# Key and query weights of a second attention, loaded and centred among the experts of the layer before it

## The chip, the cores and the metric

The kernel runs on one core of one Trainium2 chip. The metric is the device time of one execution in microseconds (us); of several runs the median is taken. A profile of one execution, taken by the hardware profiler, goes with the times.

## The reference

A two-layer perceiver block on float32 data: 8 samples of 64 latent rows of 512, and a context of 1601 rows of 512 for each sample. Six steps are added to x one after the other.

```python
x = x + L0_xattn(layernorm(x), ctx)     # 16 heads of 64 over 1601 context rows
x = x + L0_attn(layernorm(x))           # Fourier chunks, attention, convolutions
x = x + L0_ffn(layernorm(x))            # 8 experts, each token goes to one
x = x + L1_xattn(layernorm(x), ctx)     # 16 heads of 32 over 1601 context rows
x = x + L1_attn(layernorm(x))           # relative positions
x = x + L1_ffn(layernorm(x))            # ternary weights, 8 bit levels
```

The change lies in the third and the fourth step, with a trace in the fifth:

```python
# L0_ffn: the expert of the largest router logit, at most 128 tokens an expert
h   = gelu(layernorm(tok @ W1[e] + b1[e]) * g + b)      # 512 -> 2048
out = h @ W2[e] + b2[e]                                  # 2048 -> 512
# L1_xattn: queries and keys are normalised in each head of 32
qh = layernorm32(q @ Wq.T + bq) * q_gamma + q_beta
kh = layernorm32(ctx @ Wk.T + bk) * k_gamma + k_beta
x  = softmax(qh @ kh.T / sqrt(32)) @ (ctx @ Wv.T + bv) @ Wp.T + bp
```

## The kernel before

The kernel is written with a framework that allocates memory in pools and draws all semaphores itself. A pool is a stack-like stretch of the on-chip memory; a tile of a pool is written when the earlier users of its place are done. Pools opened later in the program take over the places of pools closed before. The framework also lays out the order of the instructions on each engine, so that the order in the source gives precedence and not the place. All stages run one after the other on the core, each in its own function.

`l0_ffn` is the layer of experts. Tokens are normalised, projected (`xf`, L1051) and routed. Each token's slot number is `key` (L1087); an indirect DMA from GpSimd writes the tokens to their slots in memory (`slots`, L1092). `gather(e)` (L1101) fetches the tokens of expert e, turned into columns (`tok`): for expert 0 by a matmul of `xf` with a comparison of slot numbers (L1116, L1119), for all others by reading `slots` and transposing (L1111, L1113). `Hidden` holds one expert's work: `block` (h_ps, L1139) makes 512 of the 2048 hidden columns, `norm` and `turn` normalise and transpose them, `out` (oe_ps, L1166) is the second matmul, whose result goes to `done` (L1171). The loop over `E_` = 8 experts runs the blocks of expert e + 1 beside the transposes and the output of expert e. `Experts.load(e)` issues the weights of an expert on SP, eight DMAs of 1 MB, into six places for w1 (four in pool `experts`, two in `c_m`) and four for w2; it is called two experts ahead. After the loop `done` is gathered back into `o` by four indirect DMAs (L1198), normalised and added to x (L1206).

`l1_xattn` is the second attention. Its pools are, from the bottom: `d_e` (`ep`: the key weight wk, its bias bk, the centring matrix c_center, and kT0), `d_c` (`cp`: five places for chunks of the transposed context), `d_sq` (`qp`: four squares), `d_v` (`vp`: the value weight wv), `d_w` (`wp`: small constants, among them c_heads, the output weight wo, the queries qb, kT1 to kT3, the values v), and more. The context of a sample comes in four chunks `CK` of 384, 384, 384 and 449 columns. Because every head's keys are normalised, the mean of each head's 32 output columns is taken out of the weights beforehand: `center_weights` (L1212) does it with three VectorE instructions for each quarter of a weight (sum L1218, scale L1219, subtract L1220). `project_keys` (k_ps, L1312) makes the keys of 128 columns, one pass for each of four column blocks c: ScalarE writes them to kT and their squares to a place of `d_sq`, and `deviations` sums the squares by head with c_heads (sum_ps, L1334) and takes the power -1/2 on GpSimd. Keys go through two PSUM banks (`d_ps_m`). After the keys of sample 0 the bias of the output is completed (bo_ps, L1365), then the queries are made (q_ps, L1385) from wq and bq, which are loaded and centred in pool `d_q`. Then come eight rounds, one for each sample: scores, softmax, values of this sample (v_ps, L1413), keys of the next, the weighted sum (acc) and, every second round, the output (out_ps, L1492).

`l1_tail` does the fifth and sixth step. Its pools `e_e` and `e_w` lie where the pools of the second attention were; its first weights are L1a_Wq, L1a_Wk and L1a_Wv (in `e_e`) and L1a_Wo (in `e_w`), all issued at L1688.

Of the kernel before, what the change touches and what calls it, by code (L numbers as in the profile page):

```python
# [21 lines left out]
P = 128  # L22
# [980 lines left out]
        self.held[e] = w1, w2  # L1003


def l0_ffn(K, x, d, experts, slots, done):

# [5 lines left out]
    with ExitStack() as es:  # L1013
# [87 lines left out]
        def gather(e):  # L1101

            b1 = rp.tile([P, HID], F32, tag="b1", name="b1")
            b2 = rp.tile([P, D], F32, tag="b2", name="b2")
            nc.scalar.dma_start(b1, bcast_rows(d["L0f_b1"][e]))
            nc.scalar.dma_start(b2, bcast_rows(d["L0f_b2"][e]))
            tok = rp.tile([P, DC, CAP], F32, tag="tok", name="tok")
            ps = pm.tile([P, DC, CAP], F32, tag="mm", name="tok_ps")
            rows = rp.tile([P, NT, P], F32, tag="rows", name="rows")
            if e:  # L1110
                nc.scalar.dma_start(rows, slots[ts(e, CAP), :].rearrange("p (c n) -> p c n", n=P))  # L1111
                for c in range(DC):
                    nc.tensor.transpose(ps[:, c, :], rows[:, c, :], K.ident)  # L1113
            else:
                for t in range(NT):
                    nc.vector.tensor_scalar(rows[:, t, :], slot, key[:, t : t + 1], None, ALU.is_equal)  # L1116
                for c in range(DC):
                    for t in range(NT):
                        nc.tensor.matmul(  # L1119
                            ps[:, c, :], lhsT=xf[:, t, ts(c, P)], rhs=rows[:, t, :], start=t == 0, stop=t == NT - 1  # L1120
                        )
            nc.vector.tensor_copy(tok, ps)
            return tok, b1, b2
# [54 lines left out]
        now.norm()  # L1178
        for e in range(E_):
            experts.load(e + 2)  # L1180
            then = Hidden(e + 1, after) if e + 1 < E_ else None
            for n in range(4):
                if then:
                    then.block(n)
                if n:
                    now.turn(n - 1)
            now.turn(3)
            if e + 2 < E_:
                after = gather(e + 2)
            if then:  # L1190
                then.norm()
            now.out()
            now = then
# [26 lines left out]
        nc.vector.tensor_sub(w3, w3, m.unsqueeze(2).to_broadcast([P, 16, DH]))  # L1220


def scale_heads(K, pool, y):

    nc = K.nc
    y3 = y.rearrange("p (h e) -> p h e", e=DH)
    sq = pool.tile([P, D], F32, tag="hl_sq", name="hl_sq")
    v = pool.tile([P, 16], F32, tag="hl_v", name="hl_v")
    r = pool.tile([P, 16], F32, tag="hl_r", name="hl_r")
    nc.scalar.activation(sq, y, AF.Square)  # L1230
    nc.vector.tensor_reduce(v, sq.rearrange("p (h e) -> p h e", e=DH), AX.X, ALU.add)
    K.root(pool, r, v, 1.0 / DH, EPS, v)
    nc.vector.tensor_mul(y3, y3, r.unsqueeze(2).to_broadcast([P, 16, DH]))
# [2 lines left out]
CK = [(0, 384), (384, 384), (768, 384), (1152, NKV - 1152)]  # L1236


def l1_xattn(K, x, d, in_last):

# [6 lines left out]
    with ExitStack() as es:  # L1247
# [11 lines left out]
        def weight(pool, name, shape, src):  # L1259
            t = pool.tile(shape, F32, tag=name, name=name)  # L1260
            nc.sync.dma_start(t, src)
# [5 lines left out]
        def load(b, i):  # L1267
            k0, n = CK[i]
            t = cp.tile([P, DC, CK[-1][1]], F32, tag="ctxT", name="ctxT")
# [33 lines left out]
        nc.tensor.matmul(ps, lhsT=center, rhs=bk, start=True, stop=True)  # L1303
        nc.vector.tensor_copy(bk, ps)

        def project_keys(ctxT, c, r):
# [61 lines left out]
        nc.vector.tensor_add(bo, bo, ps)  # L1368

        with tc.tile_pool(name="d_q", bufs=1) as tq, tc.tile_pool(name="d_l", bufs=2) as lp:  # L1370
            wq = chunked(tq, "L1x_WqT")
            bq = weight(tq, "L1x_bq", [P, D], bcast_rows(d["L1x_bq"]))
            xn = tq.tile([P, NT, D], F32, tag="xn", name="xn")
            xT = tq.tile([P, DC, B * S], F32, tag="xT", name="xT")

            nc.vector.tensor_scalar(ln[:, 0:2], ln[:, 0:2], ln[:, 2:3], DH**-0.5, ALU.mult, ALU.mult)
            center_weights(K, lp, wq, "hl_m")
            center_weights(K, lp, bq.unsqueeze(1), "hl_m")
            K.layernorm(lp, x, xn, functools.partial(K.root, lp))
            K.tokens_to_columns(ps_t, "t", xn, xT)  # L1380
            q = tq.tile([P, NT, D], F32, tag="q", name="q")
            for t in range(NT):
                ps = ps_m.tile([P, D], F32, tag="mm", name="q_ps")
                for c in range(DC):
                    nc.tensor.matmul(ps, lhsT=xT[:, c, ts(t, P)], rhs=wq[:, c, :], start=c == 0, stop=c == DC - 1)  # L1385
                nc.vector.tensor_add(q[:, t, :], ps, bq)
                scale_heads(K, lp, q[:, t, :])
                nc.vector.tensor_add(x[:, t, :], x[:, t, :], bo)
            for c in range(DC):
                ps = ps_t.tile([P, B * S], F32, tag="t", name="qT_ps")  # L1390
                for t in range(NT):
# [258 lines left out]
def l1_tail(K, x, d, w, known):  # L1650
# [324 lines left out]
def program(tc, d):  # L1975
    nc = tc.nc
    with tc.tile_pool(name="const", bufs=1) as cp, tc.tile_pool(name="memory", bufs=1, space=DRAM) as memory:
        K = Ctx(tc, cp)
        x = cp.tile([P, NT, D], F32, tag="x", name="x")
        nc.sync.dma_start(x[:, 0, :], d["x"][:P])  # L1980
        w = TernaryWeights(K, cp, memory, d)
        slots, done = (memory.tile([CAP * E_, D], F32, tag=n, name=n) for n in ("slots", "done"))
        l0_xattn(K, x, d, w)
        with tc.tile_pool(name="experts", bufs=4) as ep:
            experts = Experts(K, ep, d)
            wg = cp.tile([P, DC, E_], F32, tag="L0f_Wg", name="L0f_Wg")

            def loads():
                for e in range(1, E_):
                    nc.sync.dma_start(slots[ts(e, CAP), :], d["c_zero"])  # L1990
                experts.load_projection(wg)
                experts.load(0)

            l0_attn(K, x, d, loads)
            l0_ffn(K, x, d, experts, slots, done)
        known = []
        with tc.tile_pool(name="early", bufs=NT - 1) as sp:
            l1_xattn(K, x, d, lambda: known.extend(K.statistics(sp, x[:, t : t + 1, :]) for t in range(NT - 1)))
            l1_tail(K, x, d, w, known)


# [91 lines left out]
```

## Time and profile before

| What | Value |
|---|---|
| Time, median of 3 runs | 3249.63 us (3246.26 to 3250.2) |
| Profiled execution, own time | 3247.4 us |
| Its span | 3245.6 us |
| TensorE (PE) busy | 3118.5 us, 96% |
| VectorE (DVE) busy | 1751.6 us, 54% |
| GpSimd (POOL) busy | 995.1 us, 31% |
| ScalarE (ACT) busy | 848.7 us, 26% |
| DMA over the span | 336.87 MB, 104 GB/s |

The span holds, in order: the first attention to about 1500 us, the Fourier step to 1600, the experts to 1891, the second attention to about 3085, and the last two steps. In the lists of the profile PE is TensorE's matmul, PEld its loading of weights, SP the engine that issues most DMAs; SPq and ACTq are the queues of issuing instructions. "a <- b" in a list of waits reads: a waited for b. A float32 matmul shows as two records. L1312 is line 1312 of the kernel before. The granted clock (PEclk) is the share of full speed that TensorE was allowed.

### The profile page before, as it was taken

What the parts mean: (1) busy time and instruction counts of PE and PEld (TensorE: products, weight loads), DVE (VectorE), ACT (ScalarE), POOL (GpSimd) and SP (SyncE); (2) the same over time, 40 slices, a digit from 0 to 9 for tenths busy, and PEclk for the clock granted to TensorE, in tenths of its full rate; (3) what the DMA queues carried; (4) which work ended last, traced back from release to release, by engine and by line L of the source; (5) the groups of instructions that cost most, each with busy time, mean ns of one, the idle gap of its engine ahead of it and who ended that gap; (6) DMA issues with size and microseconds to landing.
All of it is one profiled execution on the core that took longest, in us unless ns stands there. A gap on an engine that the chain in (4) does not pass through costs nothing.

```text
span 3245.6 us, 39977 instructions
## 1 busy us (share of the span) xinstructions
PE 3118.5 (96%) x15601; PEld 2116.0 (65%) x15601; DVE 1751.6 (54%) x2918; ACT 848.7 (26%) x1583; POOL 995.1 (31%) x973
## 2 busy tenths in 40 slices
PE   8999999999999999999989979999999999999986
PEld 7777788888877888887344434556565555655553
DVE  5745565656566656653432345644546454454746
ACT  3232232222223222221112222323232232323323
POOL 5433325445444445440000023123141322403011
PEclk9999999999999999999989989999999999999998
DMA  8254553333455333326279650010101001000160
GB/s 261 77 170 140 157 166 113 102 93 101 137 169 160 102 126 98 106 85 215 75 268 343 236 179 20 22 31 11 41 1 41 20 22 41 1 31 1 40 137 14
DMA packets 316881, 336.87 MB, mean 104 GB/s; under 512 B 35541, under 2 KB 235733, under 8 KB 315429
## 3 DMA queue, kind: packets, MB, share of 16 engines
q1 hardware_dynamic: 310320, 316.72, 31.1%
q10 hardware_dynamic: 5733, 15.50, 1.4%
q8 instruction: 124, 2.03, 0.3%
q0 software_dynamic: 640, 2.10, 0.2%
q14 instruction: 64, 0.52, 0.0%
HBM read 308.02 MB, written 28.08 MB: 104 GB/s over the span
## 4 chain that ended last, share of the span: by engine, by line
PE 88%; DVE 5%; DMA 4%; ACT 2%; issue 1%; POOL 0%; SPq 0%; ACTq 0%; POOLq 0%; DVEq 0%
PE k_ps L1312 11%; PE v_ps L1413 11%; PE x_ps L581 10%; PE x_ps L466 9%; PE z_ps L581 4%; PE s_ps L1427 4%; PE z_ps L466 4%; PE oe_ps L1166 3%; PE h_ps L1139 3%; PE acc L1477 3%; PE y_ps L581 2%; PE y_ps L466 2%; PE sum_ps L1334 2%; PE s_ps L459 2%; DMA w_out<-wq 1%
## 5 line engine op out<-in xcount | busy, mean ns | idle before, releaser
L1349 POOL TENSOR_TENSOR r<-r,minus_half 128x24 f32<-128x24 f32 x64 | 288.7, 4515 | 712.9 <-DVE r L1345 699.9
L1312 PE MATMUL k_ps<-ctxT,L1x_WkT 128*128 128x384 f32 (+1 forms) x1024 | 381.5, 515 | 16.5 <-DVE L1x_WkT L1220 14.7
L1413 PE MATMUL v_ps<-L1x_WvT,ctxT 128*128 128x512 f32 (+1 forms) x832 | 375.0, 598 | 0.0
L466 PE MATMUL x_ps<-qt,ctxT 128*128 128x256 f32 x1152 | 286.3, 382 | 6.4 <-DVE s L431 5.1
L1312 PEld LDWEIGHTS k_ps<-ctxT,L1x_WkT 128*128 128x128 f32 x1024 | 186.0, 192 | 160.8 <-issue 46.9
L581 PE MATMUL x_ps<-pt,ctx 128*128 128x256 f32 x1152 | 280.3, 381 | 2.4 <-DVE a L559 1.3
L1413 PEld LDWEIGHTS v_ps<-L1x_WvT,ctxT 128*128 128x128 f32 (+1 forms) x832 | 148.3, 186 | 169.2 <-issue 163.4
L466 PEld LDWEIGHTS x_ps<-qt,ctxT 128*128 128x128 f32 x1152 | 216.9, 190 | 47.6 <-DVE s L431 9.2
L581 PEld LDWEIGHTS x_ps<-pt,ctx 128*128 128x128 f32 x1152 | 216.5, 189 | 36.0 <-DVE a L556 1.6
L137 POOL TENSOR_TENSOR ctxT<-ctxT 128x256 f32<-128x256 f32 x96 | 76.6, 798 | 405.8 <-DMA ctxT<-in_ctxT 367.7
L1427 PEld LDWEIGHTS s_ps<-qb,kT 64*128 64x128 f32 x1664 | 143.4, 187 | 74.4 <-DVE s L1439 44.4
L447 DVE TENSOR_TENSOR m<-m,s 128x512 f32<-128x512 f32 x176 | 134.6, 765 | 94.7 <-ACT s L445 92.1
L137 POOL TENSOR_TENSOR ctx<-ctx 128x256 f32<-128x256 f32 x96 | 72.5, 755 | 346.4 <-DMA ctx<-in_ctx 290.7
L1427 PE MATMUL s_ps<-qb,kT 64*128 64x128 f32 x1664 | 170.5, 287 | 7.0 <-DVE s L1439 6.8
L1316 ACT ACTIVATE kT<-k_ps,L1x_bk 128x384 f32<-128x384 f32 (+1 forms) x128 | 75.9, 593 | 356.8 <-PE k_ps L1312 343.5
L1345 DVE TENSOR_SCALAR r<-sumT_ps 128x12 f32<-128x12 f32 (+1 forms) x128 | 16.5, 166 | 252.0 <-PE sumT_ps L1342 251.7
L1416 ACT COPY v<-v_ps 128x512 f32<-128x512 f32 (+1 forms) x104 | 60.5, 582 | 330.5 <-PE v_ps L1413 330.5
L1439 DVE TENSOR_TENSOR s<-s_ps,r 128x512 f32<-128x512 f32 x192 | 124.7, 683 | 32.1 <-PE s_ps L1427 31.7
L499 DVE TENSOR_TENSOR s<-s,top_ps 128x1024 f32<-128x1024 f32 (+1 forms) x112 | 123.3, 1137 | 20.5 <-PE top_ps L489 20.5
L1468 DVE TENSOR_TENSOR s<-s,top_ps 128x1664 f32<-128x1664 f32 x64 | 117.9, 1884 | 27.6 <-PE top_ps L1464 27.6
L1447 DVE TENSOR_TENSOR fold<-s 128x1536 f32<-128x1536 f32 x64 | 112.1, 1751 | 37.5 <-ACT s L1469 37.4
L431 DVE SCALAR_TENSOR_TENSOR s<-y_ps,bias,p 128x256 f32<-128x256 f32 x96 | 46.3, 482 | 140.6 <-PE y_ps L466 140.4
(416 smaller groups left out, 5664.4 us busy)
## 6 DMA issues: line engine op xcount, KB each, us to landing
w<-in_L0f_W SPq DMA_DIRECT2D x64, 1024.0 KB, 7.5
ctxT<-in_ctxT SPq DMA_DIRECT2D x192, 256.0 KB, 4.6
ctx<-in_ctx SPq DMA_DIRECT2D x192, 256.0 KB, 3.2
ctxT<-in_ctxT SPq DMA_DIRECT2D x24, 768.0 KB, 4.4
wvT<-in_L0x_WvT SPq DMA_DIRECT2D x16, 1024.0 KB, 8.0
qk<-qk_all SPq DMA_DIRECT2D x15, 1024.0 KB, 7.1
qk_all<-stage SPq DMA_DIRECT2D x32, 384.0 KB, 3.4
wraw<-in_L1f_w1T SPq DMA_DIRECT2D x16, 512.0 KB, 4.3
```

Of the source, the lines that this page charges most:

```text
L137: nc.gpsimd.tensor_add(q[:, 4, :], q[:, 2, :], q[:, 3, :])
L447: nc.vector.tensor_max(self.m, self.m if k else self.s[:, LAST, :], self.s[:, k, :])
L466: nc.tensor.matmul(ps, lhsT=ctxT[i][:, Quarters.LEFT[n], ts(e, P)], rhs=right[n][:, e, :], start=start and e == 0, stop=e == 1, skip_group ...
L499: nc.vector.tensor_sub(s[:, k : k + n], s[:, k : k + n], top.unsqueeze(1).to_broadcast([P, n, HALF]))
L581: nc.tensor.matmul(ps, lhsT=ctx[pair][:, Quarters.LEFT[n], ts(m, P)], rhs=right[n][:, i, :], start=start and i == 0, stop=i == 2, skip_gro ...
L1312: nc.tensor.matmul(ps[:, :n], lhsT=wk[:, e, ts(c, P)], rhs=ctxT[i][:, e, :n], start=e == 0, stop=e == DC - 1)
L1349: nc.gpsimd.tensor_tensor(r[:, at : at + n, :], r[:, at : at + n, :], minus_half[:, :n, :], ALU.pow)
L1413: nc.tensor.matmul(ps[:kn], lhsT=ctxT[i][:, c, ds(at, kn)], rhs=wv[:, c, :], start=c == 0, stop=c == DC - 1)
L1427: nc.tensor.matmul(pair[j][:, i, :], lhsT=kT[c][rows, ts(k0 + i, P)], rhs=qb[rows, c, b].rearrange("p h q -> p (h q)"), start=True, stop=True,
L1439: nc.vector.tensor_mul(out, in_, by)
L1447: nc.vector.tensor_tensor(t, s[:, :, 0:6, :], s[:, :, 6:12, :], op)
L1468: nc.vector.tensor_sub(s[:, j], s[:, j], ps[:, j, :].unsqueeze(1).to_broadcast([P, NK, P]))
```

## The change

A new class `Ahead` holds the key weight, its bias, the centring matrix, the query weight, its bias and the first two chunks of sample 0's context, in two pools that lie at the other end of the on-chip memory (`side="right"`): `keys` and `queries`. They are opened before the layer of experts. At expert 1 its `load` issues seven DMAs on SP, and at expert 3 its `center` centres wk, wq and bq. In the second attention nothing of this is loaded or centred; the first two chunks are read by the first keys from `queries`, and loaded a second time into `d_c`, after chunks 2 and 3, because the values need them later. The pool `queries` is closed after the queries are made, `keys` before the last steps.

With that go three smaller edits. `gather` makes the tokens of expert 1 by matmul as those of expert 0, so that slots of experts 0 and 1 are not zeroed. In `d_w`, kT1 to kT3 are placed first and qb before wo. The pools `e_e` and `e_w` of the last steps are opened with `reuse_waits="tile"`, which lets a tile wait for the tiles whose places it takes; the default is the pool, which waits for all pools whose memory it reaches.

```diff
-            if e:
+            if e > 1:
                 nc.scalar.dma_start(rows, slots[ts(e, CAP), :].rearrange("p (c n) -> p c n", n=P))
...
                 for t in range(NT):
-                    nc.vector.tensor_scalar(rows[:, t, :], slot, key[:, t : t + 1], None, ALU.is_equal)
+                    nc.vector.tensor_scalar(
+                        rows[:, t, :], slot, float(CAP * e), key[:, t : t + 1], ALU.add, ALU.is_equal
+                    )
...
             experts.load(e + 2)
+            if e == 1:
+                ahead.load()
+            if e == 3:
+                ahead.center()
...
+class Ahead:
+    def __init__(self, K, d, keys, queries):
+        self.K, self.d, self.pool, self.queries = K, d, keys, queries
+
+    def load(self):
+        nc, d = self.K.nc, self.d
+
+        def weight(pool, name, shape, src):
+            t = pool.tile(shape, F32, tag=name, name=name)
+            nc.sync.dma_start(t, src)
+            return t
+
+        def chunks(src):
+            return src.rearrange("(c p) n -> p c n", p=P)
+
+        self.wk = weight(self.pool, "L1x_WkT", [P, DC, D], chunks(d["L1x_WkT"]))
+        self.bk = weight(self.pool, "L1x_bk", [P, DC], d["L1x_bk"])
+        self.across = weight(self.pool, "c_center", [P, P], d["c_center"])
+        self.wq = weight(self.queries, "L1x_WqT", [P, DC, D], chunks(d["L1x_WqT"]))
+        self.bq = weight(self.queries, "L1x_bq", [P, D], bcast_rows(d["L1x_bq"]))
+        self.ctxT = [
+            weight(self.queries, f"ctxT{i}", [P, DC, n], chunks(d["ctxT"][0, :, k0 : k0 + n])) for i, (k0, n) in enumerate(CK[:2])
+        ]
+
+    def center(self):
+        for w in self.wk, self.wq, self.bq.unsqueeze(1):
+            center_weights(self.K, self.pool, w, "mean")
...
-def l1_xattn(K, x, d, in_last):
+def l1_xattn(K, x, d, ahead, queries_done, in_last):
...
-        wk = chunked(ep, "L1x_WkT")
-        bk = weight(ep, "L1x_bk", [P, DC], d["L1x_bk"])
-        center = weight(ep, "c_center", [P, P], d["c_center"])
-        ctxT = [load(0, i) for i in range(4)]
+        wk, bk = ahead.wk, ahead.bk
+        ctxT = [place() for _ in range(4)]
+        for i in (2, 3, 0, 1):
+            load(0, i, ctxT[i])
+        kT = [(wp if c else ep).tile([P, NK * P], F32, tag=f"kT{c}", name="kT") for c in range(DC)]
         sel = weight(wp, "c_heads", [P, 64], d["c_heads"])
...
+        qb = wp.tile([P, DC, B, 2, S], F32, tag="qb", name="qb")
         wo = chunked(wp, "L1x_Wp")
         bo = weight(wp, "L1x_bp", [P, D], bcast_rows(d["L1x_bp"]))
-
-
-        qb = wp.tile([P, DC, B, 2, S], F32, tag="qb", name="qb")
-        kT = [(wp if c else ep).tile([P, NK * P], F32, tag=f"kT{c}", name="kT") for c in range(DC)]
...
-        center_weights(K, ep, wk, "mean")
         ps = ps_t.tile([P, DC], F32, tag="t", name="bk_ps")
-        nc.tensor.matmul(ps, lhsT=center, rhs=bk, start=True, stop=True)
+        nc.tensor.matmul(ps, lhsT=ahead.across, rhs=bk, start=True, stop=True)
...
-            project_keys(ctxT, c, r_of[c])
+            project_keys(ahead.ctxT + ctxT[2:], c, r_of[c])
...
-            wq = chunked(tq, "L1x_WqT")
-            bq = weight(tq, "L1x_bq", [P, D], bcast_rows(d["L1x_bq"]))
+            wq, bq = ahead.wq, ahead.bq
...
-            center_weights(K, lp, wq, "hl_m")
-            center_weights(K, lp, bq.unsqueeze(1), "hl_m")
...
+        queries_done()
...
-        ep = es.enter_context(tc.tile_pool(name="e_e", bufs=1))
-        wp = es.enter_context(tc.tile_pool(name="e_w", bufs=1))
+        ep = es.enter_context(tc.tile_pool(name="e_e", bufs=1, reuse_waits="tile"))
+        wp = es.enter_context(tc.tile_pool(name="e_w", bufs=1, reuse_waits="tile"))
...
-                for e in range(1, E_):
+                for e in range(2, E_):
                     nc.sync.dma_start(slots[ts(e, CAP), :], d["c_zero"])
...
-            l0_ffn(K, x, d, experts, slots, done)
+            keys, queries = ExitStack(), ExitStack()
+            ahead = Ahead(
+                K, d,
+                keys.enter_context(tc.tile_pool(name="keys", bufs=1, side="right")),
+                queries.enter_context(tc.tile_pool(name="queries", bufs=1, side="right")),
+            )
+            l0_ffn(K, x, d, experts, slots, done, ahead)
...
-            l1_xattn(K, x, d, lambda: known.extend(K.statistics(sp, x[:, t : t + 1, :]) for t in range(NT - 1)))
+            l1_xattn(K, x, d, ahead, queries.close, in_last)
+            keys.close()
```

More of the change, by code (lines that the diff above doesn't have):

```diff
@@ L1003, in load, with l0_ffn @@
         self.held[e] = w1, w2
-def l0_ffn(K, x, d, experts, slots, done):
+def l0_ffn(K, x, d, experts, slots, done, ahead):
     tc, nc = K.tc, K.nc
@@ L1265, in chunked, with place, load @@
             return weight(pool, name, [P, DC, D], d[name].rearrange("(c p) n -> p c n", p=P))
-        def load(b, i):
+        def place():
+            return cp.tile([P, DC, CK[-1][1]], F32, tag="ctxT", name="ctxT")
+        def load(b, i, t=None):
             k0, n = CK[i]
-            t = cp.tile([P, DC, CK[-1][1]], F32, tag="ctxT", name="ctxT")
+            t = t or place()
             nc.sync.dma_start(t[:, :, :n], d["ctxT"][b, :, k0 : k0 + n].rearrange("(c p) n -> p c n", p=P))
             return t
-        wk = chunked(ep, "L1x_WkT")
-        bk = weight(ep, "L1x_bk", [P, DC], d["L1x_bk"])
-        center = weight(ep, "c_center", [P, P], d["c_center"])
-        ctxT = [load(0, i) for i in range(4)]
+        wk, bk = ahead.wk, ahead.bk
[3 more added lines that the diff above has]
+        kT = [(wp if c else ep).tile([P, NK * P], F32, tag=f"kT{c}", name="kT") for c in range(DC)]
         sel = weight(wp, "c_heads", [P, 64], d["c_heads"])
@@ L1994, in program, with in_last @@
             l0_attn(K, x, d, loads)
-            l0_ffn(K, x, d, experts, slots, done)
+            keys, queries = ExitStack(), ExitStack()
[5 more added lines that the diff above has]
+            l0_ffn(K, x, d, experts, slots, done, ahead)
         known = []
         with tc.tile_pool(name="early", bufs=NT - 1) as sp:
-            l1_xattn(K, x, d, lambda: known.extend(K.statistics(sp, x[:, t : t + 1, :]) for t in range(NT - 1)))
+            def in_last():
+                known.extend(K.statistics(sp, x[:, t : t + 1, :]) for t in range(NT - 1))
+            l1_xattn(K, x, d, ahead, queries.close, in_last)
+            keys.close()
             l1_tail(K, x, d, w, known)
```

## The prediction

> **What bounds the kernel now.** I read the page first. Its line of busy times, with the share of the span in brackets, says that one engine sets the pace:
>
> ```profile
> PE 3118.5 (96%) x15601; PEld 2116.0 (65%) x15601; DVE 1751.6 (54%) x2918; ACT 848.7 (26%) x1583; POOL 995.1 (31%) x973
> ```
>
> So only PE's gaps, 127 us in all, and PE's work itself are worth anything. The waits of PE, one view around the first expert and one around the first keys (us in total, times, longest), show the gaps that the change can reach:
>
> ```profile
> PE tok_ps L1113 <- DMA rows<-slots: 8.2, 1, 8.2
> ```
>
> ```profile
> PE k_ps L1312 <- DVE L1x_WkT L1220: 14.7, 2, 10.9
> PE bk_ps L1303 <- DMA c_center<-in_c_center: 6.9, 1, 6.9
> ```
>
> The first is expert 1's rows, still travelling through memory. The others are the second attention, which loads and centres its key weights only when the last expert is over. The chain of waits there (start, length, what):
>
> ```profile
> 1883.72 7.31 PE oe_ps L1166 x17
> ...
> 1891.78 5.79 DMA done<-oe
> ...
> 1899.80 6.13 DMA o<-done,index
> ...
> 1913.69 4.77 DMA L1x_WvT<-in_L1x_WvT
> 1918.46 3.41 DVE mean L1219
> 1921.87 0.04 DVE hl_m L1218
> 1921.91 0.70 DVE L1x_WkT L1220
> 1922.65 1.65 PE k_ps L1312 x2
> ```
>
> The experts end at T = 1891.05, and keys flow from 1922.65. What the new order still has to wait for is in SP's waits and in POOL's timeline:
>
> ```profile
> SPq L1261 <- DVE x L1206: 3.0, 1, 3.0
> ```
>
> ```profile
> 1917.54 0.32 POOL L1293 MEMSET kT<- 128x63 f32 x3 [14.11 <-DVE x L1206]
> ```
>
> The first load (c_heads) and first memsets in pool d_w go only after the last use of the experts' memory, the sum into x at L1206. kT0 lies in d_e and was cleared at 1891.08. Last, three stretches (length, busy us of PE, PEld, DVE, ACT, POOL with counts, granted clock, DMA share, GB/s):
>
> ```profile
> 1520.00:1524.00 4.00, 4.00 (x27) 3.08 (x27) 0.84 (x2) 0.00 (x0) 0.00 (x0) 1.00 1.04 387
> 1746.30:1776.30 30.00, 30.00 (x86) 13.72 (x85) 8.56 (x13) 7.04 (x17) 0.55 (x1) 1.00 0.97 341
> 1891.05:1922.65 31.60, 8.25 (x14) 3.68 (x14) 19.60 (x54) 2.09 (x5) 9.15 (x13) 0.60 0.78 264
> ```
>
> A round of one expert has a full PE with DMA at 341 GB/s, near the 387 it reached at 1520; the gap has PE idle for 23 us and the clock at 0.60.
>
> **The change part by part.** Times are of the profiled execution: 3247.4 us, with 1.8 of it outside the span of 3245.6, and 2.2 under the median.
>
> *Expert 1's tokens by matmul.* Four transposes that wait 8.16 us give way to 16 products, 32 records. From the end of tok_ps of expert 0 (1639.1) to the second run of h_ps (1657.81) PE spends 18.7 us: 0.8 idle, 8.85 on 20 records of h_ps, 8.16 idle, 0.9 on transposes. Without the wait it is 32 records plus the same 8.85. The same 32 records for expert 0 took 6.07 us (1633.04 to 1639.11) at a clock of 0.5 to 0.8; 32 records of k_ps L795 took 3.57 at full clock. The clock is 1.00 from 1640, so I take 3.7: 12.5 us, saving 6.2. After the wait, 28 records ran in 13.90 us where the full clock takes 12.04: 1.9 more. Together 8.1, bounds 5.7 and 8.4. Four more comparisons on DVE (0.28 us each) lie beside PE's tok_ps of expert 0; one zero-fill fewer on SP is nothing. What is late next: w1 of expert 1, third block, whose place comes free at about 1646 and which lands 7.4 us later (median of the expert loads), 10 us before its use.
>
> *Loads among the experts.* Seven DMAs on SP: two weights (1.05 MB each), bias, bk, c_center and two chunks (0.79 MB each), 3.9 MB, 10.1 us at 387 GB/s. Issuing costs SP about 4.6 us (0.4 each, 1.06 a chunk), beside waits of 113 us for oe_ps. An engine's order is not the source's: the memset of L1196, written behind the expert loop, ran at 1654.69. So the loads go somewhere between 1601, when the first block's memory comes free, and expert 3.
> Among the experts they push weight loads back by up to 10.1 us. The first w2 place comes free at 1714.20 and is read at 1740.40: 26.2 us less 7.4 (at most 11.1) to land leaves 15 us or more, so nothing. The cover goes if the delay passes 15 us; then PE waits one to one. A round's spare, 46 GB/s for 30 us, is 1.4 MB: drained in three rounds.
> At 1601 they fall into a hole (0 GB/s from 1612 to 1620), but 1 MB ahead of c_slot costs it up to 2.7 us, and ACT's copy of xT waited for c_slot until 1608.11. Between 0 and 5 I take 1.5 lost, nearer to zero, as one weight before c_slot is the closest row.
> The Trainium skill ("DMA: Bandwidth & Descriptors", Bandwidth) speaks against the change: it has transfers from HBM bound at about 358 GB/s per core. The row of 387 disagrees and decides. By 358, as an estimate, the delay would be 10.9 us and drain at 0.5 MB a round, to the experts' end; still under 15, so the sum is the same with less margin.
>
> *Centring among the experts.* 27 DVE instructions, nine of each kind at 0.69, 0.18 and 0.69 us: 14 us, against 21 free in each round. Hidden; if it stood ahead of a bias sum, h_ps has four banks (13.8 us) of cover.
>
> *The start of the keys.* PE's work from there to bo_ps is four passes of 13.39 us (1934.83 to 1948.22, full clock, sums included) and 3.9 of bo_ps: 57.5. It took 87.7 (1891.05 to 1978.78). Now wk is ready, and PE begins when the last oe_ps bank is read, T + 0.75. Chunks 0 and 1 are there; chunk 2 is the first DMA after T and lands in 5 us (WkT, 1 MB, took 5.7 from the same state), as 5.2 us of chunks 0 and 1 end; chunk 3 follows in time. Pass 0 needs only kT0 and the four sq tiles. Then two chunks of pass 1 fill both ps_m banks: 48 records, 16.3 us, and PE stands at T + 17, because kT1, c_heads and so the sums lie in d_w. Behind the waiting k_ps are all later matmuls. d_w opens with L1206, T + 26.2 before; the DVE chain loses the six centring instructions in it (2.6 us), so T + 23.6; with SP's issue and the 2.1 us of a small load (c_past) the sums run at T + 26.4. Of 57.5, 41.2 remain; the clock falls in a gap of 9.4 us and costs about 2.7 (it stood at 0.5 from 1922.65 to 1928). End at T + 70.3 against T + 87.7: 17.4 saved. Bounds: 10 (d_w as late as before, only pass 0 done ahead) and 30 (no wait on d_w). The reload of chunks 0 and 1 and WvT stand ahead of c_heads on SP, 4.3 MB with chunks 2 and 3, through by about T + 13; POOL's memset of qb, 3.5 us, stays behind d_w.
>
> *The tail.* With wk gone, e_e reaches into the memory of d_w, which is free only after out_ps (L1a_Wo was issued at 3084.94, L1a_Wq at 3040.82). Waiting tile by tile keeps L1a_Wq where it was: kT1 was last read long before. Zero; between -3 and +8.4 lost.
>
> Sum: 8.1 - 1.5 + 17.4 = 24.0. 3247.4 - 24 = 3223.4; from the median, 3225.6.
>
> **The rivals.**
> 1. *No wait on d_w*: keys run through, 30 instead of 17.4, 3213. For it: the order of kT and qb was changed. Against: c_heads waited for L1206 and not just for the bytes under it.
> 2. *The front pays*: early loads hold ACT's copies and centring stands in DVE's queue ahead of the router, whose small steps have no cover. The first part loses 3 instead of gaining 6.6: 3235. Against: DMA is empty from 1612.
> 3. *The tail pays*: L1a_Wq waits for d_w as a whole. Without its 12.6 us of q_ps PE reaches out_ps's end at 3072.3, then 5.7 of load and 2.7 of half clock: 8.4 lost, 3234. It is also the case that the new waits do not do what they say.
> 4. *Slower: the eight rounds of samples get longer.* Every order is laid out anew. Rounds take 138.3 and 141.7 us with 0.9 idle; PE waits for DVE 5.5 us in 840. If one fold of the softmax (1.75 + 0.96 + 3 x 0.43 = 4.0 us of DVE) comes late in every round, eight rounds lose 32: 3257.6. It decides from 3.0 us a round. Against: a round's instructions and buffers are unchanged, and DVE is busy for only 71 of 138.
>
> **How the numbers follow.** Forecast 0.58; rivals 0.10, 0.10, 0.07 and 0.11; 0.04 for something near zero. About 0.2% (6.5 us) can be told from no change. Faster is the first four, 0.85; same 0.04; slower 0.11. From 3212 to 3240 lie the forecast, its bounds and rivals 1 to 3, which leaves about 0.15 out.
>
> **What would show it.** Right: no wait of tok_ps for rows near 1650; rounds still at 30 us with PE full; k_ps within 1 us of the last oe_ps; then one gap of about 9 us before the third chunk of pass 1, ended by c_heads or kT1; L1a_Wq not later against v_ps. Wrong: rounds of over 30 us (DMA has no slack), a keys phase without a gap, q_ps of the tail waiting for L1a_Wq, or rounds of samples off 138.3 and 141.7.

## The result

The changed kernel takes 3244.87 us (median of 20 runs, 3237.64 to 3252.94), the kernel before, run beside it, 3248.57 us (20 runs). The ratio is 0.999, with a 95% interval of 0.9983 to 0.9997: 3.7 us are gained where 24 were forecast, and the time lies outside the forecast range of 3212 to 3240. Single executions spread over 15 us. The profiled one has an own time of 3252.94 us, eight over the median, so stretches of the profiles are compared below, and each with a second profile of the same kernel (`after_again`). Line numbers are those of the kernel that is shown.

The page's line of busy times shows nothing of where the gain went: PE is busy for 3122.9 us, 96% as before.

The waits of PE from 1600 to 1720 (us in total, times, longest). The wait of tok_ps for rows is gone; in its place h_ps waits for a bias sum of DVE, and the router's matmuls wait for DVE longer than before:

```profile
PE h_ps L1141 <- DVE h L1144: 5.5, 1, 5.5
...
PE rank_ps L1080 <- DVE one L1072: 2.9, 1, 2.9
PE xt_ps L107 <- DVE xfT L51: 2.8, 1, 2.8
```

Behind the wait of h_ps stands the clearing of o (L1196 before, L1202 after), which DVE has ahead of that bias sum. o takes the place of xf, so the clearing waits until the four scatters have read xf. DVE's timeline shows it before and after. After, the trace puts the wait down to a weight's transfer; the fourth scatter, issued at 1659.20, landed half a microsecond ahead of the clearing:

```profile
1654.69 1.76 DVE L1196 MEMSET o<- 128x2048 f32 x1 [9.64 <-DMA slots<-xf,index]
```

```profile
1666.16 1.76 DVE L1202 MEMSET o<- 128x2048 f32 x1 [16.18 <-DMA w<-in_L0f_W]
```

DVE's timeline in the router (start, length, engine, line, operation, in brackets the idle time ahead and what ended it). The centring (L1224 to L1226) stands among the router's steps (L1052, L1068 on), far ahead of expert 3, beside which the source has it. DVE even idles 2.81 us for the key weight, and the second bias sum of xf comes at 1617.50 instead of 1615.45:

```profile
1610.60 0.69 DVE L1052 TENSOR_TENSOR xf<-xf_ps,L0f_bp 128x512 f32<-128x512 f32 x1 [3.31 <-PE xf_ps L1051]
1614.10 0.69 DVE L1224 TENSOR_REDUCE mean<-L1x_WkT 128x16 f32<-128x512 f32 x1 [2.81 <-DMA L1x_WkT<-in_L1x_WkT]
...
1617.50 0.68 DVE L1052 TENSOR_TENSOR xf<-xf_ps,L0f_bp 128x512 f32<-128x512 f32 x1
...
1634.60 0.18 DVE L1225 TENSOR_SCALAR mean<-mean 128x16 f32<-128x16 f32 x1
1634.70 0.19 DVE L1069 TENSOR_TENSOR one<-logit,top 128x32 f32<-128x32 f32 x1
1634.81 0.69 DVE L1226 TENSOR_TENSOR L1x_WqT<-L1x_WqT,mean 128x512 f32<-128x512 f32 x1
```

The rounds of the experts are as before: from 1739 to 1769 PE is busy for all 30.00 us at a granted clock of 1.00, with 340 GB/s.

PE at the keys: k_ps begins 0.8 us after the last oe_ps (1897.5), as forecast, but it stops twice, the first time for ScalarE, the second time for c_heads and, after four records of sum_ps, for ScalarE again:

```profile
1898.30 11.03 PE L1352 MATMUL k_ps<-ctxT,L1x_WkT 128*128 128x384 f32 x32 [0.67 <-DVE oe L1172]
1915.96 7.33 PE L1352 MATMUL k_ps<-ctxT,L1x_WkT 128*128 128x384 f32 x16 [6.64 <-ACT sq L1357]
1924.87 0.87 PE L1374 MATMUL sum_ps<-sq,c_heads 128*64 128x384 f32 x4 [1.57 <-DMA c_heads<-in_c_heads]
1928.77 1.65 PE L1352 MATMUL k_ps<-ctxT,L1x_WkT 128*128 128x384 f32 x2 [3.04 <-ACT sq L1357]
```

In ScalarE's list a root of the experts' last normalisation (L66), which waits for VectorE, stands ahead of the eviction of a chunk of keys (L1356), though that chunk's k_ps was done by 1909.33:

```profile
1913.35 0.20 ACT L66 ACTIVATE root_t<-lt_var 128x1 f32<-128x1 f32 x1 [7.23 <-DVE lt_var L65]
...
1914.88 0.56 ACT L1356 ACTIVATE kT<-k_ps,L1x_bk 128x384 f32<-128x384 f32 x1
```

The later stop of 3.04 us has the same form: a root at 1928.04 had waited 3.92 us for VectorE. There an instruction of the queries' normalisation (xn) took 3.47 us beside GpSimd's clearing of qb; the next one of the same size took 0.53:

```profile
1923.82 3.51 POOL L1337 MEMSET qb<- 128x4096 f32 x1
1924.13 3.47 DVE L83 TENSOR_SCALAR xn<-x,lt_mv,lt_rstd 128x512 f32<-128x512 f32 x1
```

And PE where the last steps begin, first before, then after the change. Before, the transposes and queries of the last steps (xt_ps, q_ps) ran in the gaps of the last softmax, ahead of out_ps; now they follow it:

```profile
3057.92 0.66 PE L1715 MATMUL xt_ps<-ident,xn 128*128 128x128 f32 x4
...
3077.23 4.14 PE L1720 MATMUL q_ps<-xT,L1a_Wq 128*128 128x384 f32 x12
3081.20 3.60 PE L1492 MATMUL out_ps<-L1x_Wp,oT 128*128 128x512 f32 x8
```

```profile
3067.82 3.70 PE L1530 MATMUL out_ps<-L1x_Wp,oT 128*128 128x512 f32 x8 [2.81 <-DVE oT L1590]
3072.75 0.66 PE L1753 MATMUL xt_ps<-ident,xn 128*128 128x128 f32 x4 [1.24 <-DVE xn L83]
...
3076.68 12.28 PE L1758 MATMUL q_ps<-xT,L1a_Wq 128*128 128x384 f32 x32 [0.68 <-ACT xT L1754]
```

q_ps does not wait for its weight: L1a_Wq was issued at 2976.82. It waits for xT, so for xn, which DVE makes directly after its sum into x (L1537):

```profile
3071.55 0.69 DVE L1537 TENSOR_TENSOR x<-x,out_ps 128x512 f32<-128x512 f32 x1 [3.79 <-PE out_ps L1530]
3072.16 0.54 DVE L83 TENSOR_SCALAR xn<-x,lt_mv,lt_rstd 128x512 f32<-128x512 f32 x1
```

All profiles by stretch, in us: router from the first xt_ps of the experts to rank_ps, experts from there to the end of the last oe_ps, keys from there to the end of bo_ps, last steps from the end of the last v_ps to the end of the span. Between keys and last steps lie the rounds of samples, 1061.5 to 1062.0 in every profile: they never changed.

| Kernel | router | experts | keys | last steps |
|---|---|---|---|---|
| before | 26.5 | 260.9 | 87.7 | 204.9 |
| after, first profile | 34.2 | 260.9 | 73.7 | 218.0 |
| after_again | 34.6 | 253.8 | 73.7 | 214.0 |
| late_centre | 26.4 | 252.2 | 73.4 | 217.2 |
| late_clear | 34.1 | 252.5 | 73.1 | 213.4 |
| late_both | 27.9 | 252.9 | 73.8 | 217.9 |
| before_gather | 26.4 | 255.3 | 89.3 | 208.7 |
| before_gather_late_clear | 25.9 | 252.7 | 87.7 | 203.9 |
| before_y3 | 26.3 | 261.2 | 87.8 | 218.0 |
| y_above | 34.3 | 254.0 | 73.7 | 204.3 |
| pool_waits | 35.1 | 253.3 | 73.4 | 217.3 |
| low_keys | 34.0 | 261.5 | 66.8 | 204.2 |
| powers_alone | 34.9 | 253.7 | 70.3 | 218.0 |
| front_tail_keys | 26.1 | 252.5 | 66.5 | 207.4 |
| all_and_powers | 27.9 | 251.3 | 65.3 | 204.2 |
| as_forecast | 26.4 | 252.2 | 73.3 | 203.9 |

So the change wins 14 us at the keys and loses some 8 in the router and 9 to 13 in the last steps; the 7 that the experts can win are there in some executions and not in others.

### The profile page after: what moved, and what is told of

Same layout as the page of the kernel before. It is cut to its first block, busy times and chain, and to the rows that moved or that the text cites. A ratio compares the mean times of both kernels' runs of the same rounds, so it can differ in the third digit from the quotient of the medians.

```text
span 3251.2 us, 40038 instructions
## 1 busy us (share of the span) xinstructions
PE 3122.9 (96%) x15623; PEld 2123.5 (65%) x15629; DVE 1757.9 (54%) x2922; ACT 850.1 (26%) x1583; POOL 997.8 (31%) x973
## 4 chain that ended last, share of the span: by engine, by line
PE 87%; DVE 6%; DMA 4%; ACT 2%; issue 1%; POOL 0%; SPq 0%; ACTq 0%; DVEq 0%; POOLq 0%
PE v_ps L1451 11%; PE k_ps L1352 11%; PE x_ps L581 10%; PE x_ps L466 9%; PE z_ps L466 4%; PE s_ps L1465 4%; PE z_ps L581 4%; PE oe_ps L1168 3%; PE h_ps L1141 3%; PE acc L1515 3%; PE y_ps L581 2%; PE y_ps L466 2%; PE sum_ps L1374 2%; PE s_ps L459 1%; PE v_ps L614 1%; PE qk_ps L252 1%
## 5 line engine op out<-in xcount | busy, mean ns | idle before, releaser
L1356 ACT ACTIVATE kT<-k_ps,L1x_bk 128x384 f32<-128x384 f32 (+1 forms) x128 | 75.9, 594 | 351.4 <-PE k_ps L1352 349.3
L1141 PE MATMUL h_ps<-w,tok 128*128 128x512 f32 x256 | 120.3, 605 | 5.5 <-DVE h L1144 5.5
```

The source lines that it names most:

```text
L1141: nc.tensor.matmul(ps, lhsT=self.tok[:, c, :], rhs=self.w1[n][:, c, :], start=c == 0, stop=c == DC - 1)
```

## The experiments

**The front.** Run first: the changed kernel again.

> The changed kernel as it is, once more, as the measure for the other runs beside it. Its first profile stood at 3252.9 us, eight above the median of its runs. If the front (the router's chain on VectorE and the scatters of tokens) varies from one execution to the next, the stretch from the first xt_ps of the experts to the last oe_ps differs from the 295.1 us of that profile (before: 287.4) and the rest stays: keys 73.7 us from the last oe_ps to the end of bo_ps (before 87.7), last v_ps to the end of out_ps 38.3 us with q_ps behind it. If the spread lies elsewhere, the front is 295 again. Median expected at 3245, a few us under the kernel before.

Measured: ratio 0.9998 (0.9984 to 1.0012), median 3246.99 us; from the first xt_ps to the last oe_ps 288.3 us instead of 295.1. By this interval the change as a whole can't be told from no change. The wait of h_ps is absent. So that part of the front does vary by execution, while the router's 34.6 us do not.

Next, the centring held back. `issue_after` puts the instructions of its block behind the given one on that one's engine; `then.last` is the bias sum that `block` has just made.

```diff
-            if e == 3:
-                ahead.center()
...
+            if e == 2:
+                with tc.issue_after(then.last.ins):
+                    ahead.center()
```

> The changed kernel with one thing altered: the 27 centring instructions are queued on VectorE behind the last bias sum of expert 3, where the source has them, and no longer stand among the router's steps. Theory (the centring pays in the front): the router's chain ends some 7.5 us earlier, as before, so from the first xt_ps of the experts to the last oe_ps 295.1 falls to about 288, and the time by 5 to 8 us. The wait of h_ps for the bias sum behind the clearing of o stays, some 3 to 6 us. Rival (the loads themselves hold ScalarE's copies and the DMA queues, the order on VectorE does not matter): the stretch stays at 295 and the time is the same within 1.5 us.

Measured: ratio 0.9965 (0.9947 to 0.9982), 3238.64 us. The router takes 26.4 us as in the kernel before, although the early loads were issued as before (the key weight at 1606.93): the loads cost nothing, the place of the centring on VectorE cost 8.1 (34.6 less 26.4, unrounded). Run at 1730 to 1748, beside a full PE, the same centring cost nothing that shows (experts 252.2). In this execution h_ps did not wait for the clearing either, which had been expected to stay.

```diff
+            if e == E_ - 2:
+                behind = now.sum
...
-        nc.vector.memset(o, 0.0)
+        with tc.issue_after(behind.ins):
+            nc.vector.memset(o, 0.0)
```

Here `now.sum` is the sum that `out` makes into oe, so `behind` is that of expert 6.

> The changed kernel with one thing altered: the clearing of o (which takes the place of xf and so waits for the four scatters out of xf) is queued on VectorE behind the output sum of expert 6, no longer ahead of the first bias sums. Theory (the wait for rows has turned into this one, behind the same scatters): the wait of h_ps for DVE, 5.5 us in the profile, goes, and with it 4 to 6 us of the stretch and of the time. Rival (h_ps waits since the tokens come late in any case): the wait is replaced by another on PE, for rows of expert 2 or for weights, and the time stays within 1.5 us.

Measured: ratio 0.9983 (0.9973 to 0.9994), 3244.47 us. No wait of h_ps, experts 252.5 us. The interval overlaps that of `after_again`, so the runs' times don't show the gain; the profiles do, for here the scatters took as long as in the first profile of after (the last one was issued 6.5 us after the third) and PE was not held.

> The changed kernel with both: centring behind the bias sums of expert 3, clearing of o behind the output of expert 6. If the two theories hold and add, the stretch from the first xt_ps of the experts to the last oe_ps is 295.1 - 7.5 - 5.5 = about 282 us, 5 under the kernel before, which is the gain that tokens of expert 1 by matmul were forecast to bring; the time falls by 10 to 13 us against the changed kernel as it is, to about 3233. If only one of them holds, by 5 to 7. Keys and last steps are not touched and stay at 73.7 us, and with q_ps behind out_ps.

Both edits together: 0.9963 (0.9951 to 0.9975), 3238.84 us, router and experts 280.8. About 8 us came instead of 10 to 13. Against `late_centre` the clearing adds nothing that the runs can tell.

**Why the moved wait comes and goes.** Four scatters leave GpSimd one after the other, each when the one before has landed, and the clearing of o waits for the last. The timelines of GpSimd and of SP, after (first profile):

```profile
1652.83 0.97 POOL L1092 DMA_INDIRECT slots<-xf,index  x1 [2.04 <-DMA slots<-xf,index]
1659.20 0.97 POOL L1092 DMA_INDIRECT slots<-xf,index  x1 [5.40 <-DMA slots<-xf,index]
```

```profile
1652.72 10.67 SPq L997 DMA_DIRECT2D w<-in_L0f_W  x4
```

and in `after_again`:

```profile
1652.08 0.97 POOL L1092 DMA_INDIRECT slots<-xf,index  x1 [2.04 <-DMA slots<-xf,index]
1655.13 0.97 POOL L1092 DMA_INDIRECT slots<-xf,index  x1 [2.08 <-DMA slots<-xf,index]
```

```profile
1653.47 17.53 SPq L997 DMA_DIRECT2D w<-in_L0f_W  x6
```

Where SP issued the next weights within 0.3 us of the third scatter (after, `late_clear`, `low_keys`, `all_and_powers`), the fourth scatter followed 6.35 to 6.7 us after the third; where it issued them 0.7 to 1.5 us later (ten profiles), 3.0 to 3.9 us after it. In the kernel before and in `before_y3`, with the weights 1.7 us ahead, it was 4.4 and 4.9. That the weights' packets hold up the scatter's is the likely reading; no run set the one against the other alone.

**The tokens by matmul alone**, on the kernel before:

> The kernel before with the tokens of expert 1 by matmul alone (three edits of the change: the branch of the gather, the comparison with CAP times e, one zero-fill less). Forecast of the prediction for this part: 8.1 us saved, bounds 5.7 and 8.4; from the first xt_ps of the experts to the last oe_ps 287.4 falls to 279 to 281.5. Rival (the wait for rows becomes the wait for the clearing of o behind the same scatters): it saves 2 to 4 us at most, 284 to 286, with a wait of h_ps for DVE of 3 to 6 us. Keys and last steps as before.

Measured: 0.9965 (0.9953 to 0.9977), 3239.28 us, 12 us under before by the medians. In the profile router and experts fell from 287.4 to 281.8 us, and PE waited once: h_ps for the bias sum of DVE, 2.5 us. So 5.6 us, and 8.1 without that wait. The profiled execution is the slowest of the seven (3247.19 us), so its stretches show less than the runs. With the clearing behind expert 6:

> The kernel before with the tokens of expert 1 by matmul and the clearing of o behind the output of expert 6. In the run without the second edit h_ps waited 2.5 us for the clearing, and 5.6 us were saved up to the last oe_ps. Theory (the wait on the scatters had moved to the clearing): this wait goes, and from the first xt_ps of the experts to the last oe_ps 287.4 falls to 279 to 280, the 8.1 of the prediction. Rival (the 2.5 us are taken by another wait, for rows of expert 2 or a weight of expert 1): 281 to 282.

Measured: 0.9972 (0.9962 to 0.9983), 3237.73 us; the wait is gone, router and experts take 278.6 us, 8.8 less than before. The step is worth what the sum said, and a part of it can be taken by the second wait on the same scatters.

**The last steps.** The kernel before with y larger by one place, which moves the end of e_e above the start of d_w and touches no other stage. By the shapes of the tiles e_e takes 66000 bytes of a partition; d_w begins at 66736 in the kernel before and at 57952 in the changed one. One more place of y makes e_e 70160 bytes:

```diff
-            y = ep.tile([P, 2, DC, 2, S + 1], F32, tag="y", name="y", bufs=2)
+            y = ep.tile([P, 2, DC, 2, S + 1], F32, tag="y", name="y", bufs=3)
```

> The kernel before with one number altered: tile y of the last steps has three places instead of two, so that pool e_e is 4160 bytes larger and ends above the start of pool d_w, as it does in the changed kernel. Nothing of the experts or the keys is touched. Theory (the tail pays because e_e reaches into d_w, whatever the way of waiting: the order on every engine is laid out as if the first normalisations had to wait for out_ps): the first q_ps comes after the end of out_ps, the stretch from the last v_ps to the end of the span grows from 204.9 us to 214 to 218, and the time by 9 to 13. Rival (the loss comes from waiting tile by tile or from closing the new pools, not from the place): the stretch stays at 205 and the time within 2 us of the kernel before.

Measured: 1.0038 (1.0026 to 1.005), 3263.8 us, 12 us slower; last steps 218.0 us, with q_ps behind out_ps:

```profile
3078.79 3.70 PE L1492 MATMUL out_ps<-L1x_Wp,oT 128*128 128x512 f32 x8 [2.81 <-DVE oT L1552]
3083.95 0.63 PE L1715 MATMUL xt_ps<-ident,xn 128*128 128x128 f32 x4 [1.46 <-DVE xn L83]
...
3088.90 6.47 PE L1720 MATMUL q_ps<-xT,L1a_Wq 128*128 128x384 f32 x10 [1.73 <-DMA L1a_Wq<-in_L1a_Wq]
```

The reverse, on the changed kernel, allocates y from `wp` (e_w) instead of `ep`, which leaves e_e 57680 bytes:

> The changed kernel with one thing altered: tile y lies in e_w instead of e_e, so that e_e ends below d_w again. Centring and keys stay as they are. Theory (the place decides): first normalisations and q_ps go back between the steps of the last softmax, the stretch from the last v_ps to the end falls from 214 to 218 us to about 205, the time by 9 to 13 against the changed kernel, to about 3235. Rival (waiting tile by tile makes the order): nothing moves, 3245 to 3247.

Measured: 0.9944 (0.9924 to 0.9965), 3235.52 us; last steps 204.3, and q_ps begins 15 us before out_ps again:

```profile
3054.10 2.85 PE L1758 MATMUL q_ps<-xT,L1a_Wq 128*128 128x384 f32 x8 [0.67 <-ACT xT L1754]
...
3068.83 3.60 PE L1530 MATMUL out_ps<-L1x_Wp,oT 128*128 128x512 f32 x8
```

Both ways the place of one tile decides. Is it the manner of waiting?

```diff
-        ep = es.enter_context(tc.tile_pool(name="e_e", bufs=1, reuse_waits="tile"))
-        wp = es.enter_context(tc.tile_pool(name="e_w", bufs=1, reuse_waits="tile"))
+        ep = es.enter_context(tc.tile_pool(name="e_e", bufs=1))
+        wp = es.enter_context(tc.tile_pool(name="e_w", bufs=1))
```

> The changed kernel with the pools e_e and e_w opened in the default way, so that they wait for whole pools and not for tiles. The order on VectorE and TensorE is the same as in the changed kernel; only the waits differ. Theory (the order already puts the first normalisations behind out_ps, so tile-wise waiting can bring only the loads forward): L1a_Wq is issued after out_ps instead of 57 us before the end of the keys' rounds, q_ps waits some 3 to 6 us for it, and the stretch from the last v_ps to the end grows from 214 to 218 us to 218 to 224; the time is 3 to 6 us over the changed kernel. Rival (the loads are covered by the half-empty stretch after out_ps): within 2 us.

Measured: 0.999 (0.9979 to 1.0001), 3247.48 us, as the changed kernel; last steps 217.3. L1a_Wq is now issued after out_ps, but q_ps waits only 1.0 us for it:

```profile
3073.51 12.03 PE L1758 MATMUL q_ps<-xT,L1a_Wq 128*128 128x384 f32 x32 [1.03 <-DMA L1a_Wq<-in_L1a_Wq]
```

The rival held. With either manner of waiting xn stands directly behind the sum into x on DVE. Waiting tile by tile, as used here, removed a wait and left the order.

**The keys.** What the second pass needs goes under the experts' weights, into d_v, which opens with the last oe_ps; wv goes to d_w, y to e_w:

```diff
-        kT = [(wp if c else ep).tile([P, NK * P], F32, tag=f"kT{c}", name="kT") for c in range(DC)]
+        kT = [(ep, vp, wp, wp)[c].tile([P, NK * P], F32, tag=f"kT{c}", name="kT") for c in range(DC)]
...
-        wv = chunked(vp, "L1x_WvT")
+        wv = chunked(wp, "L1x_WvT")
```

and c_heads, minus_half, last_sums, the tiles of `sums` and `r` from `vp` in the same way.

> The changed kernel with y in e_w, and with what the second pass of keys needs (kT1, c_heads, last_sums, minus_half, the sums and the powers r) moved into pool d_v, which lies under the experts' weights and opens with the last oe_ps; the value weight wv goes to d_w in exchange. Theory (the gaps of the keys are the wait for d_w, about 5 us with its clock, and ScalarE's root of the experts' normalisation ahead of the eviction of keys, 6.6): the wait for c_heads goes, the first gap stays; from the last oe_ps to the end of bo_ps 73 falls to 64 to 68, and the time stands 5 to 9 under that of y_above. Rival (both gaps come from the experts' end on VectorE and ScalarE, memory is no matter): the stretch stays at 71 to 73, the time equals y_above. If all gaps went it would be 57.5 to 60.

Measured: 0.9947 (0.9929 to 0.9964), 3233.83 us. Keys 66.8 us instead of 73.7, and of the two gaps only the first is left:

```profile
PE k_ps L1352 <- ACT sq L1357: 6.6, 1, 6.6
```

The time stands only 1.7 us under `y_above`, well inside the intervals, where 5 to 9 were expected. In this profile the front was the longer one (experts 261.5, h_ps waiting 5.5).

Then the two normalisations at the end of the experts and ahead of the queries take their root as a power on GpSimd (the argument `functools.partial(K.root, lp)` left out in both), on the changed kernel:

> The changed kernel with only those two roots as powers on GpSimd. Theory (in the changed kernel the wait for d_w, which opens some 25 us after the last oe_ps, ends last, and the gap behind the root lies inside it): the first gap goes and the second one, ended by c_heads or kT1, grows by as much, so that there is the single gap of 8 to 11 us that was forecast, and from the last oe_ps to the end of bo_ps there are still 70 to 74 us; the time is the same within 3 us. Rival (the root is the whole reason why the keys came out shorter of the forecast): 66 to 68 us, and 6 to 7 us off the time.

Measured: 0.9981 (0.9968 to 0.9993), 3244.6 us; keys 70.3 us. PE's timeline is the one that the prediction had drawn: 48 records, then a single gap.

```profile
1893.31 16.19 PE L1352 MATMUL k_ps<-ctxT,L1x_WkT 128*128 128x384 f32 x48 [0.67 <-DVE oe L1172]
1918.39 1.55 PE L1374 MATMUL sum_ps<-sq,c_heads 128*64 128x384 f32 x4 [8.89 <-DMA c_heads<-in_c_heads]
```

The roots had cost 3.4 us beyond the wait for d_w, and most of the first gap lay inside that wait: counted from the last oe_ps the sums begin at 25.9 us instead of 27.4. The stop after them is 0.7 us instead of 3.0; here no xn runs beside the clearing of qb. The runs' times do not tell this kernel from the changed one, as expected.

**All together.** `front_tail_keys` has the late centring, the late clearing and the places of `low_keys`.

> Three repairs together on the changed kernel: centring behind the bias sums of expert 3, clearing of o behind the output of expert 6, and the places of low_keys (y in e_w; kT1, c_heads and the sums of the keys in d_v). By the parts: the front saves 8 us against the changed kernel, the keys 7, the last steps 9 to 13, so 24 to 28 in all, about 3220 and 28 under the kernel before; this is the forecast of the prediction with the value weight and the keys of the second pass not waiting for d_w. Stretches: from the first xt_ps of the experts to the last oe_ps about 279, to the end of bo_ps 66 to 68, last v_ps to the end 204 to 209. Rival (the parts get into each other's way, since every order is laid out anew): less than 20 saved against the kernel before.

Measured: 0.9897 (0.9881 to 0.9914), 3220.21 us, about 31 under the kernel before by the medians. The parts add.

> As front_tail_keys, and the roots of the experts' last normalisation and of that of the queries are taken as powers on GpSimd instead of square roots on ScalarE. Theory (the gap of 6.6 us that is left in the keys is ScalarE, which holds the eviction of the third chunk behind a root that waits for VectorE): from the last oe_ps to the end of bo_ps 67 falls to 58 to 61, and the time by 6 to 8 more, to about 3213. Rival (the evictions wait for something else, or GpSimd's clearing of qb takes the place of ScalarE's root): 65 to 67 and the time of front_tail_keys.

Measured: 0.9895 (0.9878 to 0.9911), 3216.65 us; keys 65.3 us, so the expectation of 58 to 61 was wrong and the rival's 65 to 67 right. The gap behind the root went, and the next engine in order took its place: the statistics of x on VectorE stand ahead of the instructions that read the sums of the keys.

```profile
PE sumT_ps L1386 <- DVE lt_mv L97: 5.0, 2, 3.4
```

Last, whether the places found are all of the miss: late centring, late clearing and y in e_w, the keys left as the change has them.

> The changed kernel with the two steps repaired at which the prediction is thought to have failed, and nothing else: centring behind the bias sums of expert 3 and clearing of o behind the output of expert 6, so that neither stands ahead of work on VectorE that is waited for, and y in e_w, so that e_e ends below d_w. Keys stay as in the changed kernel. If these steps are all of the miss, the sum of the prediction holds but for the keys (13.9 instead of 17.4): 8.1 + 13.9 = 22 us under the kernel before, 21 to 24, ratio 0.9927 to 0.9935; from the first xt_ps of the experts to the last oe_ps 279, to the end of bo_ps 73 to 74, last v_ps to the end 204 to 209. If something else in the changed kernel costs time that the profiles do not show, less than 18 us is saved.

Measured: 0.9924 (0.9909 to 0.9939), 3224.26 us. The forecast for the change was 3225.6. By stretch: router and experts 278.6 (8.8 saved), keys 73.3 (14.4), last steps 203.9 (1.0), about 24 us together. That this is the forecast's 24.0 is in part luck: the front gave 2.2 more than the 6.6 forecast, the last steps 1.0 more than nothing, and the keys 3.0 less than 17.4.

## Why the prediction was wrong

**Centring among the experts, taken as hidden.** This step failed. 27 centring instructions were put at nothing; they cost about 8 us. Their cover was looked up where the source has it, in a round with 21 us of free VectorE, and there `late_centre` shows it to hold. The same prediction had said that an engine's order is not the source's, and had placed the loads by it, between 1601 and expert 3; it did not do so for the centring, which became ready as soon as its weight had landed. It stood among small steps of the router that nothing covers. Rival 2 named this place at a chance of 0.10, beside a loss by the early loads that didn't come; it priced the first part at 3 us lost, and `after_again` shows 0.9 lost, the first profile 7.7.

**Expert 1's tokens by matmul.** The size was right: 8.1 forecast, 8.8 measured with the clearing out of the way. Asked what is late next, the prediction named a weight. It was the clearing of o, whose wait of 9.64 us for the same scatters was in the trace of before, hidden under the wait for rows. It took 5.5 us of PE in the first profile and nothing in the second.

**The loads.** 1.5 us were charged; `late_centre`, with the loads as early, shows a router of 26.4 us against 26.5: nothing. Rounds of the experts stayed full, as forecast.

**The keys.** 17.4 forecast, 14.0 measured. Start, order of the passes and the gap at d_w were right, as `powers_alone` shows: end at T + 70.3, as the sum said, with a gap of 8.9 us where 9.4 was said. The term that was missing is ScalarE's queue: two gaps instead of one, 3.4 us. The prediction let GpSimd's clearing of qb stand behind d_w at no cost. Its own chain of before has a sign of that cost, a scaling of the centring (mean, L1219) that took 3.41 us beside this clearing, where the prediction counted 0.18 for each.

**The last steps, taken at zero.** This step failed for 9 to 13 us, the largest single error. PE's idle time in the last steps is 37.7 to 37.9 us in all eight profiles with q_ps ahead of out_ps, and 47.9 to 49.5 in all eight with q_ps behind it. The prediction saw that e_e reaches into d_w and asked only when the weight L1a_Wq comes; that was earlier than before. What moved was the normalisation and with it 12 us of q_ps, which had filled PE's gaps in the last softmax. Rival 3 had this loss of cover at 8.4 us and a chance of 0.07, but by way of a late weight; `pool_waits` shows that with q_ps behind out_ps a late weight adds at most 1.0. That the framework lays out the order as if whole pools were waited for is an inference: the runs show that it depends on whether e_e reaches d_w, and is the same for both manners of waiting.

**Rival 4**, longer rounds of samples, didn't come: 1061.9 and 1062.0 us. Rival 1, no wait on d_w, describes `low_keys`, not the change; even there the keys save 20.9 us and not 30, as ScalarE's gap stays.

The last steps of some executions are about 4 us longer with the same waits on PE (204 against 207 to 209, 214 against 217 to 218). It lies in PE's busy time, not in its waits: after's two profiles have PE idle for 48.8 and 48.3 us, but busy for 169.1 at a mean granted clock of 0.88 and for 165.7 at 0.90. A lower clock is the likely reading; why it was granted is open.

## What to carry to other kernels

Work that is moved early is placed by a scheduler such as this one where its inputs become ready, not where the source has it: ask what stands behind it on its engine at the earliest moment it can run, and hold it back by an explicit order if that work has no cover. When a tile leaves a stack of pools, everything above it slides; look up which later pool now reaches into one that ends late, since that alone cost 12 us here. And when a wait on a chain of transfers is taken away, look for the next instruction that waits for the same chain.

## What was not expected of the hardware

Four scatters in a row, of the same data, ended earlier or later from one execution to the next. The step from the third to the fourth was 3.05 us where the weights were issued 1.4 us after the third, and 6.37 us where they were issued 0.1 us ahead of it. The clearing that waits for all four began 20.4 us after the first scatter's issue in the one and 25.7 in the other. The two profiles of one kernel differ by 7 us in the experts, 5.5 of them the wait of h_ps; that the order of issue decides it is argued from 16 profiles and not tested alone.

The clearing of qb on GpSimd (3.51 us) held some instructions of VectorE until about its end: xn took 3.47 us beside it in the eight profiles where it began during the clearing, 4.51 in the two where it began 0.16 us ahead of it, and 0.53 to 0.55 otherwise. Statistics of 0.68 us ran beside it unharmed in `all_and_powers`. The runs don't show why.
